# Two layers of attention and experts: products of the identity in front of instructions that TensorE waits for

## The chip, the cores and the metric

The kernel runs on one core of one Trainium2 chip. The metric is the device time of one execution in microseconds (us), as a median of several runs. A profile of one execution stands beside it. In the text, PE is TensorE, DVE is VectorE, ACT is ScalarE, POOL is GpSimd and SP is SyncE. "L1247" is line 1247 of the kernel before the change.

## What is computed

Two transformer layers follow each other on an input of 4 batches, 1024 rows and 256 columns, in float32. Each layer is an attention and a mixture of experts, both with a norm, a shift, a scale and a gate from a small modulation product. Cut to what matters:

```python
x = x + ga * attention0(norm(x) * (1 + ca) + sa)      # 16 heads, causal softmax, latent k and v
x = x + gb * experts0(norm(x) * (1 + cb) + sb)        # 16 experts, the best 2 of each row
x = x + ga1 * attention1(norm(x) * (1 + ca1) + sa1)   # linear attention with cubed q and k, a convolution of 3 rows
x = x + gb1 * experts1(norm(x) * (1 + cb1) + sb1)     # 8 experts, the best one of each row

def experts0(x):   # the reference computes all experts and picks two
    h = gelu(norm(x @ W1[e] + b1[e]) * g1[e] + be1[e])
    return sum(weight[e] * (h @ W2[e] + b2[e]) for e in best_two)
```

## The kernel before

The kernel does not compute all experts. It sorts the rows by expert: rows are written to DRAM, scattered by POOL's indirect DMAs into tiles of 128 rows that all belong to one expert, multiplied by that expert's weights, and gathered back. The tile's expert is a number in a register, so the weight is addressed at run time.

The stages follow each other as attention 0, experts 0, attention 1, experts 1. They overlap: what an object called `Around` holds (norms, routing, sorting, scattering, combining, each a Python generator cut into pieces) is traced in small pieces between the matmuls of the running stage. `k.around.step(pieces)` takes some pieces. A compiler then orders each engine's instructions by a schedule of its own, earlier code first among what is ready. `k.pin(ins)` fixes one order: the instruction stands behind the one that was traced last on the same engine. Each engine runs its instructions in that order.

Results of TensorE go to tiles in PSUM. A pool gives a tag a number of buffers; a new tile takes the buffer of an old one and waits until all readers of the old tile are done.

What the change touches:

- `Sorting.sort` ranks the rows of each expert (`ps_rank`, L895, read by DVE at L899 and L901). DVE then works out where each expert's tiles begin (L904 to L947). A product `ps_expert` (L949) counts the experts before each tile, and DVE turns that into an offset (L950). It serves both layers: in experts 0 for two halves of the batches (`hf`), in experts 1 for three parts (`p`: batches 0 and 1, batch 2, batch 3).
- `routed_rows` normalises a batch for the experts: ACT or DVE write `h` (L1030 to L1046), TensorE transposes it (`ps_lnT`, L1057), ACT copies it (L1063 or L1068), and `route_logits` multiplies by the router (L794) and turns the logits (L802, read at L803).
- `Experts0.run` walks through 22 groups of 4 tiles, 11 of each half. For a group, `arrive` transposes the sorted rows (`ps_xT`, L1224, copied by ACT at L1230). `hidden` multiplies by W1 (`ps_h`, L1247), and DVE adds the bias and takes the statistics (L1255 to L1263). `normalised` is on ACT (L1270). `turned` transposes (`ps_hT`, L1286) and applies the gelu on ACT (L1295). `output` multiplies by W2 (`ps_y`, L1312), and DVE adds the bias (L1321). Each tag has 2 buffers, and a group takes two of them. In a round, `turned` of group n-2, `hidden` of group n, `arrive` of group n+1 and `output` of group n-2 are traced in this order. At the switch to the second half (`second_half`), `arrive` comes after `output`, since the rows must have been scattered. The pools for `ps_xT` also serve `k.misc` (`ps_lnT`, `ps_route`, `ps_logits`, `ps_rank`, `ps_expert`).
- `attention1` runs `front(b)` and `back(b-1)` side by side. `front` transposes the norm (`ps_lnT`, L153), multiplies by the weights of k and v (`ps_k`, L1511) and of q (`ps_q`, L1537). `back` has `ps_o` (L1574), its transposes `ps_oT` (L1589), the convolution (L1597 on ACT, L1601 on DVE) and the projection `ps_pr` (L1609). The norms and sorts of experts 1 are traced in pieces between them.

Of the kernel before, what the change touches and what calls it, by code (L numbers as in the profile page):

```python
# [8 lines left out]
F32 = mybir.dt.float32  # L9
# [6 lines left out]
P = 128  # L16
# [49 lines left out]
def bcast(ap, axis, n):  # L66

    shape = list(ap.shape)
    shape.insert(axis, n)
    return ap.unsqueeze(axis).to_broadcast(shape)  # L70

# [771 lines left out]
class Sorting:  # L843
# [38 lines left out]
    def sort(self, sel, pool, index, offset):  # L882
# [65 lines left out]
        pe = k.misc.tile([1, self.tiles], F32, tag="m", name="ps_expert")  # L948
        nc.tensor.matmul(pe, lhsT=self.all[:ne, 0:1], rhs=past[:, 1], start=True, stop=True)  # L949
# [67 lines left out]
def routed_rows(k, work, b, statistics, scale, shift, wr, br, ne, logits, scalar):  # L1017


    nc = k.nc  # L1020
# [31 lines left out]
    for q in range(2):  # L1052
        hT = work.tile([P, CC, 512], F32, tag="hT", name="hT", bufs=1)
        for cc in range(CC):
            ps = k.misc.tile([P, 512], F32, tag="m", name="ps_lnT")
            for i in range(4):
                tr = nc.tensor.transpose(  # L1057
                    ps[:, i * P : (i + 1) * P], h[:, i, cc * P : (cc + 1) * P], k.ident
                )
                if i == 0:  # L1060
                    k.pin(tr)
            if scale is None:
                nc.scalar.activation(  # L1063
                    hT[:, cc], ps, AF.Identity,
                    bias=k.modF[:, cc, b : b + 1], scale=k.modF[:, 2 + cc, b : b + 1],
                )
            else:
                nc.scalar.copy(hT[:, cc], ps)  # L1068
            if q == 0 and cc == CC - 1:
                h = yield from normalised(1)  # L1070
            else:
                yield 1
        yield from route_logits(k, hT, wr, br, ne, work, logits[:, 4 * q : 4 * q + 4])


class Experts0:
# [40 lines left out]
    def sort(self, hf):  # L1117

        k, rt, keep, sorting, logits = self.k, self.rt, self.keep, self.sorting, self.logits
        nc = k.nc  # L1120
# [57 lines left out]
    def run(self, early):  # L1178
# [37 lines left out]
        def arrive(tiles, xss):  # L1216

            xTs = []
            for i, xs in zip(range(0, len(tiles), 2), xss):
                m = min(2, len(tiles) - i)  # L1220
                ps = ps_x.tile([P, 2, CC, P], F32, tag="m", name="ps_xT")
                for j in range(m):
                    for cc in range(CC):
                        tr = nc.tensor.transpose(  # L1224
                            ps[:, j, cc], xs[:, j, cc * P : (cc + 1) * P], k.ident
                        )
                        if j == cc == 0:
                            k.pin(tr)
# [5 lines left out]
        def hidden(hf, tiles, xTs):  # L1234
# [7 lines left out]
            for i in range(0, n, 2):  # L1242
                m = min(2, n - i)
                ph = ps_h.tile([P, 2, C], F32, tag="h", name="ps_h")
                for j in range(m):
# [58 lines left out]
        def output(hf, tiles, at, acts):  # L1304

            n = len(tiles)
            for i in range(0, n, 2):
                m = min(2, n - i)
                po = ps_o.tile([P, 2, C], F32, tag="o", name="ps_y")
                for j in range(m):  # L1310
# [43 lines left out]
        for n, (hf, tiles) in enumerate(groups):  # L1354
            last = waiting.pop(0) if len(waiting) > 1 else None

            if last and n > 2:
                acts = turned(*last)
            now = hidden(hf, tiles, xTs)
# [6 lines left out]
            switch = n + 1 == most  # L1366
            if n + 1 < len(groups) and not switch:
                xTs = arrive(groups[n + 1][1], coming.pop(0))
# [10 lines left out]
            if switch:  # L1379
                xTs = arrive(groups[n + 1][1], coming.pop(0))  # L1380
# [8 lines left out]
        normalised(*final)  # L1389
        output(*last[:3], acts)  # L1390
# [54 lines left out]
def attention1(ctx, k, a, after_batch=lambda b: None):  # L1445
# [48 lines left out]
    def front(b):  # L1494
# [13 lines left out]
        for t in range(NT):  # L1508
            ps = ps_p.tile([P, 512], F32, tag="p", name="ps_k")
            for cc in range(CC):  # L1510
                k.anchor = nc.tensor.matmul(  # L1511
                    ps, lhsT=hT[:, cc, t * P : (t + 1) * P], rhs=wqkv[:, cc, C:],
                    start=cc == 0, stop=cc == CC - 1,
                ).ins
# [269 lines left out]
class Experts1:  # L1784
# [42 lines left out]
    def rows(self, b):  # L1827

        k, rt = self.k, self.rt
        part = next(p for p in PARTS if b in p)  # L1830
# [15 lines left out]
    def sort(self, p):  # L1846

        k, rt, keep, sorting, logits = self.k, self.rt, self.keep, self.sortings[p], self.logits
# [169 lines left out]
def two_layers(ctx: ExitStack, tc: tile.TileContext, a: dict, out: bass.AP):  # L2018
# [56 lines left out]
    def stages(first, second, early):  # L2075
        for buffer in k.sorted0 + k.sorted1:
            buffer.writers.clear()
        k.around, k.statistics, k.xn, k.anchor = Around(), {}, None, None
# [108 lines left out]
```

## Time and profile before

| | us |
|---|---|
| median of 3 runs | 1098.98 |
| lowest and highest run | 1098.36, 1101.94 |
| the profiled execution | 1087.63 |
| its span, from the first to the last instruction | 1085.8 |

| engine | busy us | share of the span |
|---|---|---|
| PE | 945.7 | 87% |
| DVE | 620.4 | 57% |
| ACT | 602.5 | 55% |
| POOL | 336.0 | 31% |

The mean granted clock of TensorE is 0.955 of full speed. Attention 0 takes the span up to some 515 us, experts 0 goes to 749, attention 1 to 970, experts 1 to the end.

In lines of the timeline, the first two numbers are start and length in us, then come engine, line, operation, output and inputs, shapes and the number of records. In brackets stand the idle time of the engine before it and what ended that. In lines of stretches, the first numbers are the stretch and its length, then the busy time of PE, PE's weight loads, DVE, ACT and POOL with their records, then the granted clock, the share of the DMA engines and GB/s.

### The profile page before, as it was taken

How to read it: one execution, taken by the hardware profiler on the slowest of the kernel's cores; microseconds unless marked ns; L12 is line 12 of the kernel's file. 1: busy time of each engine (PE TensorE's matmuls, PEld its weight loads, DVE VectorE, ACT ScalarE, POOL GpSimd, SP SyncE). 2: the span in 40 equal slices, each digit the busy share in tenths (PEclk: the TensorE clock that was granted, in tenths of full speed). 3: DMA queues.
4: the chain of work that ended last, by engine and by line, in shares of the span. 5: the costliest groups of instructions: out<-in, count | busy, mean ns of one | idle time of the engine just before them, and what ended most of it. 6: DMA issues, size and time to landing. Idle time of an engine off the chain costs nothing.

```text
span 1085.8 us, 18090 instructions
## 1 busy us (share of the span) xinstructions
PE 945.7 (87%) x6072; PEld 559.8 (52%) x6072; DVE 620.4 (57%) x1987; ACT 602.5 (55%) x959; POOL 336.0 (31%) x528
## 2 busy tenths in 40 slices
PE   4899999999999999889679989986997989858760
PEld 2434434443443434335568878874464656547550
DVE  5822235422465155413676767993899968564572
ACT  0368655765477555775555657766654745523430
POOL 2013211311232234663004615612550100553632
PEclk9999999999999999999899999998999899989875
DMA  6995000100010001552825556624223201458764
GB/s 206 358 346 179 1 1 6 40 1 1 1 64 1 1 30 54 201 215 78 317 88 170 197 177 189 196 75 144 67 65 148 88 2 39 141 170 264 240 205 130
DMA packets 97142, 132.89 MB, mean 122 GB/s; under 512 B 8536, under 2 KB 84216, under 8 KB 96528
## 3 DMA queue, kind: packets, MB, share of 16 engines
q1 hardware_dynamic: 84656, 97.27, 26.9%
q0 software_dynamic: 11776, 33.57, 9.9%
q8 instruction: 52, 0.85, 0.3%
q10 hardware_dynamic: 608, 0.79, 0.3%
q14 instruction: 50, 0.41, 0.1%
HBM read 67.85 MB, written 63.75 MB: 121 GB/s over the span
## 4 chain that ended last, share of the span: by engine, by line
PE 63%; DVE 19%; issue 5%; DMA 5%; ACT 4%; POOL 1%; SPq 1%; DVEq 0%; ACTq 0%; POOLq 0%
PE ps_s L388 13%; PE ps_av L453 12%; PE ps_qk L364 6%; PE ps_y L1312 5%; PE ps_h L1247 4%; PE ps_v L349 3%; PE ps_out L427 3%; PE ps_pr L1609 3%; PE ps_y L1938 3%; PE ps_q L1537 2%; PE ps_k L1511 2%; DVE y L1601 2%; DMA ys<-results,index 2%; PE ps_lnT L1057 1%; DVE st L1258 1%
## 5 line engine op out<-in xcount | busy, mean ns | idle before, releaser
L396 ACT ACTIVATE pT<-ps_s 128x1024 f32<-128x1024 f32 x288 | 279.3, 1022 | 169.7 <-PE ps_s L388 167.2
L399 POOL TENSOR_SCALAR_AFFINE_SELECT pT<-pT 128x256 f32<-128x256 f32 x256 | 104.2, 431 | 328.4 <-ACT pT L396 323.7
L388 PE MATMUL ps_s<-qT,kT 32*128 32x512 f32 (+3 forms) x1536 | 178.8, 523 | 0.1
L453 PE MATMUL ps_av<-pT,v 128*32 128x512 f32 (+3 forms) x1536 | 165.2, 497 | 9.4 <-DVE turned L411 5.6
L964 POOL DMA_INDIRECT sorted<-hs,index x96 | 96.2, 1002 | 144.9 <-PE ps_y L1312 73.0
L974 POOL DMA_INDIRECT ys<-results,index x96 | 102.7, 1070 | 119.0 <-DMA results<-y 43.6
L388 PEld LDWEIGHTS ps_s<-qT,kT 32*128 32x128 f32 x1536 | 74.5, 185 | 95.5 <-issue 72.8
L453 PEld LDWEIGHTS ps_av<-pT,v 128*32 128x32 f32 x1536 | 40.6, 108 | 104.0 <-issue 58.7
L1247 PE MATMUL ps_h<-w,xT 128*128 x352 | 82.1, 386 | 6.5 <-DVE mv L1259 3.8
L1312 PE MATMUL ps_y<-w,act 128*128 x352 | 83.7, 392 | 4.2 <-DVE rs_seed L84 2.8
L411 DVE STREAM_TRANSPOSE turned<-ps_av 128x512 f32<-128x512 f32 x32 | 22.8, 712 | 98.9 <-PE ps_av L453 98.6
L1312 PEld LDWEIGHTS ps_y<-w,act 128*128 128x128 f32 x352 | 67.7, 197 | 14.0 <-ACT act L1295 4.8
L1247 PEld LDWEIGHTS ps_h<-w,xT 128*128 128x128 f32 x352 | 66.2, 193 | 15.9 <-issue 4.2
L1295 ACT ACTIVATE act<-ps_hT,gain 128x128 f32<-128x128 f32 x176 | 63.6, 463 | 16.9 <-PE ps_hT L1286 16.8
L1270 ACT ACTIVATE hid<-hid,nmr,rstd 128x256 f32<-128x256 f32 x88 | 47.5, 603 | 39.4 <-DVE nmr L1263 39.2
L1511 PE MATMUL ps_k<-wqkv,hT 128*128 128x512 f32 x128 | 61.9, 603 | 3.6 <-DMA wqkv<-in_wqkv_dram 2.8
L1938 PE MATMUL ps_y<-we,xT 128*128 x200 | 53.0, 412 | 10.6 <-ACT xT L1930 8.4
L371 DVE COPY qT<-ps_qk 128x512 f32<-128x512 f32 x16 | 11.0, 688 | 81.8 <-PE ps_qk L364 81.8
L103 DVE BATCH_NORM_STATS2 ln_st<-x 128x6 f32<-128x256 f32 x128 | 49.2, 407 | 0.5
L1255 DVE TENSOR_TENSOR hid<-ps_h,b 128x256 f32<-128x256 f32 x88 | 33.9, 415 | 26.6 <-PE ps_h L1247 21.5
L1938 PEld LDWEIGHTS ps_y<-we,xT 128*128 128x128 f32 x200 | 38.2, 204 | 20.1 <-ACT xT L1930 11.6
L374 DVE TENSOR_SCALAR kT<-ps_qk,par 128x512 f32<-128x512 f32 x32 | 22.5, 745 | 37.0 <-PE ps_qk L364 37.0
(223 smaller groups left out, 1499.4 us busy)
## 6 DMA issues: line engine op xcount, KB each, us to landing
xs<-sorted SPq DMA_DIRECT2D x69, 256.0 KB, 3.8
results<-y SPq DMA_DIRECT2D x69, 256.0 KB, 3.0
sorted<-zero SPq DMA_DIRECT2D x2, 6016.0 KB, 20.1
rows_in<-h SPq DMA_DIRECT2D x16, 512.0 KB, 2.9
hs<-rows_in POOLq DMA_DIRECT2D x32, 256.0 KB, 3.5
w<-in_w_dram SPq DMA_DIRECT2D x8, 1024.0 KB, 11.3
x<-in_x_dram SPq DMA_DIRECT2D x4, 1024.0 KB, 6.5
b<-in_b_dram SPq DMA_DIRECT2D x2, 2048.0 KB
```

The costliest lines, as they stand in the source:

```text
L364: nc.tensor.matmul(ps, lhsT=w[:, cc, g * P : (g + 1) * P], rhs=hT[:, cc, hf * 512 : (hf + 1) * 512], start=cc == 0, stop=cc == CC - 1,)
L388: k.anchor = nc.tensor.matmul(pair[hh // 2][:, hh % 2, c0 : c0 + w], lhsT=kTs[o][rows, kb * P : (kb + 1) * P], rhs=qT[rows, q1 - w : q1], ...
L396: nc.scalar.activation(pT, ps, AF.Exp, scale=1.0 / L**0.5)
L399: nc.gpsimd.affine_select(out=pT[:, :, c0 : c0 + P], in_=pT[:, :, c0 : c0 + P], compare_op=ALU.is_ge, fill=0.0, base=0, pattern=[[0, 2], [ ...
L453: nc.tensor.matmul(po[32 * hh : 32 * hh + 32, 512 - w :], lhsT=vs[b % 2][:, kb, 8 * g + 2 * hh + o, :], rhs=exps[b, g, o, u][hh // 2][:, h ...
L964: i = self.k.nc.gpsimd.indirect_dma_start(out=buffer.ap, out_offset=bass.IndirectOffsetOnAxis(ap=index, axis=0), in_=rows, in_offset=None, ...
L974: self.paced(self.k.nc.gpsimd.indirect_dma_start(out=rows, out_offset=None, in_=buffer.ap, in_offset=bass.IndirectOffsetOnAxis(ap=index, a ...
L1247: mm = nc.tensor.matmul(ph[:, j], lhsT=xTs[i // 2][:, j, cc], rhs=w1[:, cc, bass.ds(at[i + j], C)], start=cc == 0, stop=cc == CC - 1,)
L1295: o = nc.scalar.activation(act[:, j, cc], pt[:, j, cc], AF.Gelu, bias=gain[:, 1, cc, t : t + 1], scale=gain[:, 0, cc, t : t + 1],)
L1312: mm = nc.tensor.matmul(po[:, j], lhsT=acts[i // 2][:, j, cc], rhs=w2[:, cc, bass.ds(at[i + j], C)], start=cc == 0, stop=cc == CC - 1,)
L1511: k.anchor = nc.tensor.matmul(ps, lhsT=hT[:, cc, t * P : (t + 1) * P], rhs=wqkv[:, cc, C:], start=cc == 0, stop=cc == CC - 1,).ins
L1938: k.anchor = nc.tensor.matmul(po[:, j], lhsT=xT[:, j, cc], rhs=self.we[:, cc, bass.ds(at[j], C)], start=cc == 0, stop=cc == CC - 1,).ins
```

## The change

A function `keep_warm` issues n products of the identity with itself into a PSUM tile that a following instruction then overwrites, so nobody reads them. The first is pinned. A dictionary `k.fill` holds how many are wanted under a name; the place that takes the number removes it. The code sets 16 and 20 in front of `ps_expert` of the second sort of each layer, 18, 12, 5 and 5 in front of the first `ps_lnT` of each batch for experts 1, 13 in front of `ps_h` of group 1, 12 and 9 in front of `ps_xT` of group 4 and of the first group of the second half, 9 in front of `ps_y` of the last group but one, and 10 in front of the first `ps_k`. The tile of `ps_expert` becomes 128 by 128, of which the first row is used as before. `ps_expert` in all sorts and the first `ps_k` are pinned.

```diff
--- before.py
+++ after.py
@@ -68,6 +68,15 @@
     shape = list(ap.shape)
     shape.insert(axis, n)
     return ap.unsqueeze(axis).to_broadcast(shape)
+
+
+def keep_warm(k, ps, n):
+
+
+    for i in range(n):
+        mm = k.nc.tensor.matmul(ps, lhsT=k.ident, rhs=k.ident, start=True, stop=True)
+        if i == 0:
+            k.pin(mm)
 
 
 def rsqrt(nc, pool, out, var, n, eps):
@@ -945,8 +954,10 @@
             nc.vector.tensor_scalar(past[:, i], self.numbers, edge[:, i : i + 1], None, ALU.is_ge)
         mine = pool.tile([ne, self.tiles], F32, tag="mine", name="mine")
         nc.vector.tensor_tensor(mine, past[:, 0], past[:, 1], ALU.subtract)
-        pe = k.misc.tile([1, self.tiles], F32, tag="m", name="ps_expert")
-        nc.tensor.matmul(pe, lhsT=self.all[:ne, 0:1], rhs=past[:, 1], start=True, stop=True)
+        pe = k.misc.tile([P, P], F32, tag="m", name="ps_expert")
+        keep_warm(k, pe, k.fill.pop("expert", 0))
+        pe = pe[0:1, : self.tiles]
+        k.pin(nc.tensor.matmul(pe, lhsT=self.all[:ne, 0:1], rhs=past[:, 1], start=True, stop=True))
         nc.vector.tensor_scalar(offset, pe, float(ne - 1), float(C), ALU.min, ALU.mult)
         yield 1
         return mine
@@ -1053,6 +1064,8 @@
         hT = work.tile([P, CC, 512], F32, tag="hT", name="hT", bufs=1)
         for cc in range(CC):
             ps = k.misc.tile([P, 512], F32, tag="m", name="ps_lnT")
+            if q == cc == 0:
+                keep_warm(k, ps[:, :P], k.fill.pop("rows", 0))
             for i in range(4):
                 tr = nc.tensor.transpose(
                     ps[:, i * P : (i + 1) * P], h[:, i, cc * P : (cc + 1) * P], k.ident
@@ -1116,6 +1129,8 @@
 
     def sort(self, hf):
 
+        if hf == 1:
+            self.k.fill["expert"] = 16
         k, rt, keep, sorting, logits = self.k, self.rt, self.keep, self.sorting, self.logits
         nc = k.nc
         sel = rt.tile([P, 2, HT, E0], F32, tag="sel", name="sel")
@@ -1219,6 +1234,7 @@
             for i, xs in zip(range(0, len(tiles), 2), xss):
                 m = min(2, len(tiles) - i)
                 ps = ps_x.tile([P, 2, CC, P], F32, tag="m", name="ps_xT")
+                keep_warm(k, ps[:, 0, 0], k.fill.pop("rows of tiles", 0))
                 for j in range(m):
                     for cc in range(CC):
                         tr = nc.tensor.transpose(
@@ -1242,6 +1258,7 @@
             for i in range(0, n, 2):
                 m = min(2, n - i)
                 ph = ps_h.tile([P, 2, C], F32, tag="h", name="ps_h")
+                keep_warm(k, ph[:, 0, :P], k.fill.pop("hidden", 0))
                 for j in range(m):
                     for cc in range(CC):
                         mm = nc.tensor.matmul(
@@ -1307,6 +1324,7 @@
             for i in range(0, n, 2):
                 m = min(2, n - i)
                 po = ps_o.tile([P, 2, C], F32, tag="o", name="ps_y")
+                keep_warm(k, po[:, 0, :P], k.fill.pop("output", 0))
                 for j in range(m):
                     for cc in range(CC):
                         mm = nc.tensor.matmul(
@@ -1356,6 +1374,8 @@
 
             if last and n > 2:
                 acts = turned(*last)
+            if n == 1:
+                k.fill["hidden"] = 13
             now = hidden(hf, tiles, xTs)
             if last and n == 2:
                 acts = turned(*last)
@@ -1364,6 +1384,8 @@
             if n:
                 k.around.step()
             switch = n + 1 == most
+            if n == 3:
+                k.fill["rows of tiles"] = 12
             if n + 1 < len(groups) and not switch:
                 xTs = arrive(groups[n + 1][1], coming.pop(0))
             if switch:
@@ -1377,6 +1399,7 @@
             if last:
                 output(*last[:3], acts)
             if switch:
+                k.fill["rows of tiles"] = 9
                 xTs = arrive(groups[n + 1][1], coming.pop(0))
             if n == most + 1:
                 k.around.tasks.append(self.combine(0))
@@ -1387,6 +1410,7 @@
         last, final = waiting
         acts = turned(*last)
         normalised(*final)
+        k.fill["output"] = 9
         output(*last[:3], acts)
         output(*final[:3], turned(*final))
         k.around.finish_tasks()
@@ -1507,11 +1531,16 @@
         waiting = []
         for t in range(NT):
             ps = ps_p.tile([P, 512], F32, tag="p", name="ps_k")
+            if b == t == 0:
+                keep_warm(k, ps[:, :P], 10)
             for cc in range(CC):
-                k.anchor = nc.tensor.matmul(
+                mm = nc.tensor.matmul(
                     ps, lhsT=hT[:, cc, t * P : (t + 1) * P], rhs=wqkv[:, cc, C:],
                     start=cc == 0, stop=cc == CC - 1,
-                ).ins
+                )
+                if b == t == cc == 0:
+                    k.pin(mm)
+                k.anchor = mm.ins
             r = work.tile([P, C], F32, tag="r", name="r", bufs=3)
             k3 = work.tile([P, C], F32, tag="k3", name="k3", bufs=3)
             cube(k3, ps[:, :C], r)
@@ -1827,6 +1856,7 @@
     def rows(self, b):
 
         k, rt = self.k, self.rt
+        k.fill["rows"] = (18, 12, 5, 5)[b]
         part = next(p for p in PARTS if b in p)
         i = b - part[0]
         if i == 0:
@@ -1845,6 +1875,8 @@
 
     def sort(self, p):
 
+        if p == 1:
+            self.k.fill["expert"] = 20
         k, rt, keep, sorting, logits = self.k, self.rt, self.keep, self.sortings[p], self.logits
         nc = k.nc
         nt = sorting.nt
@@ -2075,7 +2107,7 @@
     def stages(first, second, early):
         for buffer in k.sorted0 + k.sorted1:
             buffer.writers.clear()
-        k.around, k.statistics, k.xn, k.anchor = Around(), {}, None, None
+        k.around, k.statistics, k.xn, k.anchor, k.fill = Around(), {}, None, None, {}
         k.fits = [k.good[:, 3 + i : 4 + i] for i in range(SORTS)] if early else None
         experts0 = Experts0(k, a)
 
```

## The prediction, made before the change was run

> **What bounds the kernel.** First the page: engine shares, granted clock, shares of the chain that ended last.
>
> ```profile
> PE 945.7 (87%) x6072; PEld 559.8 (52%) x6072; DVE 620.4 (57%) x1987; ACT 602.5 (55%) x959; POOL 336.0 (31%) x528
> PEclk9999999999999999999899999998999899989875
> PE 63%; DVE 19%; issue 5%; DMA 5%; ACT 4%; POOL 1%; SPq 1%; DVEq 0%; ACTq 0%; POOLq 0%
> ```
>
> TensorE carries 63% of the chain, at full clock nearly everywhere. The clock falls only in single slices. Next, TensorE's waits (total, times, longest); the change aims at these:
>
> ```profile
> PE ps_expert L949 <- DVE index L933: 7.7, 1, 7.7
> PE ps_expert L949 <- DVE past L945: 6.6, 4, 4.8
> PE ps_lnT L1057 <- DVE ln_nmr L126: 5.7, 1, 5.7
> PE ps_h L1247 <- DVE mv L1259: 3.8, 1, 3.8
> PE ps_y L1312 <- DVE rs_seed L84: 2.8, 1, 2.8
> ```
>
> Third, busy time by stretches around some gaps; the clock is the number after POOL's:
>
> ```profile
> 519.70:523.50 3.80, 0.03 (x1) 0.00 (x0) 3.46 (x7) 1.26 (x3) 0.00 (x0) 1.00 1.05 414
> 523.90:527.10 3.20, 3.20 (x9) 2.57 (x8) 1.40 (x6) 0.00 (x0) 0.00 (x0) 0.50 1.03 410
> 480.60:484.00 3.40, 3.40 (x32) 1.19 (x32) 0.00 (x0) 0.92 (x1) 3.05 (x7) 1.00 0.21 76
> 633.10:636.40 3.30, 3.14 (x15) 3.17 (x16) 0.00 (x0) 1.42 (x3) 0.00 (x0) 0.50 0.92 263
> ```
>
> An idle TensorE is followed by half clock: after the 3.82 us before 523.54, and after the 2.86 us before 633.26. It is not after the 2.24 us that ended at 480.51. One such stretch costs little: 16 records of ps_h take 5.38 us at 523.54 and 3.72 at 515.14, so 1.66 us. Fourth, the timeline where two of the fills go, and where the fill for batch 2 goes:
>
> ```profile
> 522.99 0.41 DVE L1255 TENSOR_TENSOR hid<-ps_h,b 128x256 f32<-128x256 f32 x1
> 523.54 5.38 PE L1247 MATMUL ps_h<-w,xT 128*128 x16 [3.82 <-DVE mv L1259]
> ...
> 737.94 0.42 DVE L1321 TENSOR_TENSOR y<-ps_y,b 128x256 f32<-128x256 f32 x1
> 738.51 5.38 PE L1312 MATMUL ps_y<-w,act 128*128 x16 [2.83 <-DVE rs_seed L84]
> ...
> 936.79 1.63 PE L1574 MATMUL ps_o<-kv,qT 128*128 128x136 f32 x12
> 940.37 0.60 PE L1057 MATMUL ps_lnT<-ident,h 128*128 128x128 f32 x4
> ```
>
> At 523.54 TensorE starts just after VectorE's second read of an old ps_h (ends 523.40), though both input copies (ACT, L1230) ended by 520.96. With two ps_h buffers this is a wait for the **buffer**, not for the input. The same at 738.51: the second L1321 ends at 738.36, while the first activations were there by 736.6. So the wait covers both reads of the tile.
>
> **The price of a product.** No identity product is in the trace. The nearest row is ps_o (L1574): 12 records of 136 columns in 1.63 us, the last taking 0.28, so (1.63 - 0.28) / 11 = 0.12, in its even runs 0.116; for 128 columns 0.109. The code's two products per ps_o leave four records, so a product is two records: 0.22 us, 0.43 at half clock. Lower end 0.11, if it went like a transpose (L1224: 8 in 1.04). I take 0.22. The 129 products are 28 us of TensorE time, against gaps of about 40 us.
>
> **The change, place by place.** A fill writes the tile of the instruction behind it, so it needs the same buffer and starts no earlier than the buffer is free. Plus is slower.
>
> - *hidden, 13* (523.54). Buffer wait: fills start at 523.5, not in the gap. Half clock comes at 523.8 anyway. 1 product at 0.22, 8 at 0.43 until 527.2, 4 at 0.22: end 528.0. Then 16 records at 0.216 instead of the half-clock ones: end 531.5, against 528.76. **+2.8**. VectorE then idles for ps_h already (1.83 us before 527.14) and everything to 535 hangs on it, so nothing absorbs it.
> - *output, 9* (738.51): likewise. Fills to 742.0, ps_y to 745.6 against 743.72: **+1.9**, on the path into layer 1, as SyncE's loads there are queued behind the last results.
> - *rows of tiles, 12*, at group 4 (554.27). The 3.55 us wait of this line (541.28) belongs to group 3, so no gap is met. 2.6 us of fills replace a 1.15 us wait; the 1.57 us wait at 565.15 hides the rest, unless the fills also go ahead of ps_logits (554.16), which the sort on VectorE waits for (then +1.4). Between 0 and 1.4; **+0.5**.
> - *expert, 16*, first half's end (571.98, gap 4.85). The fills are pinned behind hidden's matmuls (end 563.59), not behind ps_rank (565.15) or ps_hT. In the gap as meant they end at 570.6 and ps_xT and ps_y run at full clock (1.97 to 1.04, and 2.42 to 1.92), 0.2 of it lost to a buffer: -1.2. All ahead of ps_rank they take 3.5 us where 1.57 is free: +1.9. Near the middle: **+0.3**.
> - *rows of tiles, 9*, at the switch (633.26, waits for a DMA, buffer long free): ends 632.3. Saves 0.9 + 0.7 on the two rows of 8 transposes (1.94 and 1.76, against 1.04). The start of half-clock stretches is not tied to the program; gaps this near the limit will drop in some runs only: **-0.9**, between -1.6 and 0.
> - *ps_k, 10* (756.18, waits for wqkv). Pinned behind all 16 ps_lnT, of which 6 now run after ps_k. They move into the gap, fills follow from 755.3: end 757.5 at full, 759.6 at half clock. First ps_k 1.3 to 3.4 us later, but those 6 (1.45) are done and ACT had not read it before 760.40: between -0.4 and +1.1; **+0.2**.
> - *rows 18 and 12* (842.13, 894.89): they end at 840.4 and 894.0, in the gaps, and keep the clock. But ACT is busy without a gap from 842.10 to 850 and from 895.56 to 902; it paces these stretches: **0**, between -1 and +0.5.
> - *rows 5, 5*. Batch 2 (940.37): TensorE has come straight from ps_o, no gap, and ACT L1063 sat idle 0.71 us for this tile: 5 x 0.22 = **+1.1**. Batch 3 (974.30, gap 1.72): **0**.
> - *expert, 20* (960.40, gap 7.67): 4.4 us leave 3.3 idle, enough to drop the clock again. Keeping it would save half of 3.7 us of ps_pr: 1.8. **-0.5**.
>
> Pins of ps_expert and ps_k remove freedom of order elsewhere; bounds +1 and -1, taken 0. Sum: 2.8 + 1.9 + 0.5 + 0.3 - 0.9 + 0.2 + 0 + 1.1 - 0.5 = +5.4 us. The profiled execution took 1087.63 us for a span of 1085.8, so the sum makes it 1093.0. The median of the runs, 1098.98, is 11.35 higher; I carry the difference over: 1104.4.
>
> **A rule against the trace.** After gaps of 2.83 and 2.86 us the trace has clock 0.50; after 2.24 it has 1.00. The Trainium skill ("TensorE: Matmul & The Clock Gate", "Why this matters for your kernels") tells to avoid idle over about 3 us; by that the gap at the switch would never drop the clock, its gain would be nothing and the sum +6.3. The measured rows decide. The same page's Part 4 says that transposes don't count as busy for the clock. Here the stretch from 633.10 has 15 records, all transposes, at 0.50, and the next 16 matmuls took 3.62 us, full speed. By the page the two rows at the switch would hold the clock low one stretch longer and the gain there would be 3 us; the trace decides.
>
> **Rivals.** *As meant (faster).* Every fill runs while TensorE waits, and the half-clock costs go: 1.7 + 1.2 + 1.6 + 1.7 + 1.7 + 1.8 = 9.7 us, less 1.1 for batch 2: 1090. It decides if fills at hidden and output start at 519.7 and 735.7. For it: the gaps are there and the clock does fall. Against: the buffer reads at 523.40 and 738.36. *Nothing net.* VectorE and ACT pace the stretches behind the fills, and half of the buffer delays vanishes there: 1099.5. *Order (much slower).* Products with no operand to wait for are put ahead of unready instructions: ps_rank, ps_logits, ps_lnT; +1.9, +1.4, +1.1 at their upper ends and the gains gone: 2.8 + 1.9 + 1.4 + 1.9 + 1.1 + 1.1 + 1 = 11.2: 1110. *It does not do what it says*: the clock still drops behind filled gaps, because these products count too little; 1107, part of the slower side.
>
> **Numbers.** Forecast 0.48 (its own range 1100 to 1109), as meant 0.22, nothing net 0.15, order and no effect 0.15. 0.3% is 3.3 us, about what a measurement of this kernel can tell from no change. Above 1102.3: 0.38 of the first and the last group, 0.53; below 1095.7: 0.23; between: 0.24. Range 1091 to 1111.
>
> **What would show it.** In the changed profile, fills on ps_h and ps_y that start after VectorE's second read, followed by ps_h at full clock that ends near 531.5 after a 515 start; the switch's transposes at about 1.04 us; ps_lnT of batch 2 a microsecond after ps_o. Wrong, if those fills start with the gap, or if ps_y behind them is early; the order rival shows in where ps_rank and ps_logits stand.

## The result, and the profile of the changed kernel

Changed 1099.62 us, before 1098.66 us (medians of 20 runs each), ratio 1.0012, 95% interval 0.9995 to 1.003: +1.0 us, between -0.5 and +3.3. No change that this measurement can tell; the forecast was 5.4 us slower. In two later comparisons the changed kernel was 5.3 and 5.4 us slower by the medians (e9, e13 below). In some comparisons all kernels, before included, run about 10 us shorter (before 1087 instead of 1098; one and the same chip gave 1086.69 and 1096.55). So only kernels of one comparison are set against each other. The profile of before that the prediction read (1087.63) was of the short sort, and the 11.35 us that the prediction carried over are this difference. Why the first comparison gave +1.0 and the two later ones +5.3 and +5.4 stays open.

The profiled execution of the changed kernel took 1100.96 us, its span 1099.1. Its page: engine shares, clock, shares of the chain.

```profile
PE 978.9 (89%) x6330; PEld 590.8 (54%) x6330; DVE 621.2 (57%) x1987; ACT 603.0 (55%) x959; POOL 336.0 (31%) x528
PEclk9999999999999999999999999998999899989885
PE 69%; DVE 15%; issue 5%; ACT 4%; DMA 4%; POOL 1%; another core or an unknown queue 1%; SPq 0%; DVEq 0%; POOLq 0%; ACTq 0%
```

258 matmul records more, all of them fills (129 products of two records), and 33 us of TensorE time. TensorE's waits, in the order of those shown of before (total, times, longest):

```profile
PE ps_expert L960 <- DVE past L954: 2.6, 4, 1.2
PE ps_lnT L1070 <- ACT h L1041: 4.0, 1, 4.0
PE ps_h L77 <- DVE hid L1272: 3.7, 1, 3.7
PE ps_y L77 <- DVE y L1339: 2.7, 1, 2.7
PE ps_kv L1526 <- DVE v L1551: 2.4, 1, 2.4
```

The long waits in front of ps_expert are gone: 7.7 and 4.8 us became at most 1.2. The waits in front of ps_h and ps_y are as long as before (3.8 and 2.8), but now it is the fill (L77) that waits in them. A wait of 2.4 us in front of ps_kv is longer than it was. The timeline at these places:

```profile
567.37 1.04 PE L1303 MATMUL ps_hT<-ident,hid 128*128 128x128 f32 x8
568.25 3.74 PE L77 MATMUL ps_expert<-ident 128*128 128x128 f32 x32
573.14 0.23 PE L960 MATMUL ps_expert<-past,all 16*1 16x44 f32 x2 [1.16 <-DVE past L954]
...
524.67 3.17 PE L77 MATMUL ps_h<-ident 128*128 128x128 f32 x26 [3.72 <-DVE hid L1272]
527.68 3.62 PE L1264 MATMUL ps_h<-w,xT 128*128 x16
...
745.10 3.67 PE L77 MATMUL ps_y<-ident 128*128 128x128 f32 x18 [2.74 <-DVE y L1339]
748.61 3.62 PE L1330 MATMUL ps_y<-w,act 128*128 x16
```

Ahead of ps_expert the fill stands in the gap, behind ps_hT. At hidden and output it starts only when the buffer is free, as the prediction said. Busy time and clock (the number after POOL's) in three stretches:

```profile
524.70:527.80 3.10, 3.10 (x27) 3.10 (x28) 2.84 (x14) 0.00 (x0) 0.00 (x0) 1.00 1.02 408
640.10:642.10 2.00, 1.86 (x16) 1.65 (x17) 0.00 (x0) 2.00 (x6) 0.00 (x0) 1.00 1.08 350
745.10:748.60 3.50, 3.50 (x18) 3.50 (x19) 1.95 (x12) 1.27 (x3) 0.00 (x0) 0.58 0.45 150
```

At hidden no half clock followed here, although TensorE had been idle for 3.72 us; at the switch (second row) the clock was kept; at output it was not.

Because executions differ by several us, the text goes by stretches, each between the starts of two matmul records (ps_y[16] is the 17th record that writes ps_y; records of fills are not counted). Us, in brackets us of half clock inside, all read from the traces:

| stretch | before | e1: before again | changed | e9: changed | e13: changed | e15 (the best version below) |
|---|---|---|---|---|---|---|
| ps_h[0] to ps_hT[0] (hidden 13) | 19.54 (3) | 19.10 (3) | 21.07 (0) | 22.74 (7) | 22.73 (7) | 19.46 (3) |
| ps_hT[0] to ps_y[16] (group 4) | 21.84 (3) | 21.83 (3) | 21.99 (3) | 23.02 (7) | 23.01 (7) | 21.81 (3) |
| ps_y[16] to ps_gain[8] (expert 16) | 19.80 (3) | 20.03 (3) | 17.07 (0) | 17.07 (0) | 17.09 (0) | 18.75 (0) |
| ps_gain[8] to ps_y[112] (untouched) | 42.68 (0) | 45.58 (0) | 46.17 (0) | 46.19 (0) | 45.78 (0) | 45.78 (0) |
| ps_y[304] to ps_y[336] (output 9) | 14.79 (3) | 16.15 (7) | 16.44 (3) | 16.38 (3) | 16.69 (3) | 13.10 (0) |
| ps_y[336] to ps_k[36] (ps_k 10, pin) | 45.86 (7) | 46.40 (7) | 47.86 (7) | 47.84 (7) | 49.44 (6) | 46.86 (10) |
| ps_kv[63] to ps_kv[90] (batch 0) | 52.91 (10) | 52.93 (10) | 53.98 (10) | 54.06 (10) | 53.36 (7) | 53.40 (14) |
| ps_kv[90] to ps_k[99] (batch 1) | 25.02 (3) | 25.03 (3) | 24.01 (0) | 24.02 (0) | 24.01 (0) | 24.01 (0) |
| ps_kv[126] to ps_rank[12] (batch 2) | 18.13 (0) | 18.30 (0) | 18.35 (0) | 18.34 (0) | 18.34 (0) | 18.23 (0) |
| ps_rank[12] to ps_y[416] (expert 20, batch 3) | 47.35 (10) | 47.25 (10) | 47.57 (7) | 46.60 (7) | 46.67 (4) | 43.94 (0) |

The fourth row, a stretch without fills, shows the two sorts of comparison: 42.7 us in every trace of the short one, 44.3 to 47.2 in those of the other.

### The profile page after: what moved, and what is told of

It is laid out like the page before. It is cut to its first block, busy times and chain, and to the rows that moved or that the text cites. A ratio compares the mean times of both kernels' runs of the same rounds, so it can differ in the third digit from the quotient of the medians.

```text
span 1099.1 us, 18603 instructions
## 1 busy us (share of the span) xinstructions
PE 978.9 (89%) x6330; PEld 590.8 (54%) x6330; DVE 621.2 (57%) x1987; ACT 603.0 (55%) x959; POOL 336.0 (31%) x528
## 4 chain that ended last, share of the span: by engine, by line
PE 69%; DVE 15%; issue 5%; ACT 4%; DMA 4%; POOL 1%; another core or an unknown queue 1%; SPq 0%; DVEq 0%; POOLq 0%; ACTq 0%
PE ps_s L397 14%; PE ps_av L462 13%; PE ps_y L1330 6%; PE ps_h L1264 5%; PE ps_qk L373 5%; PE ps_k L1537 4%; PE ps_out L436 3%; PE ps_pr L1638 3%; PE ps_v L358 2%; PE ps_q L1566 2%; PE ps_y L1970 2%; PE ps_lnT L1070 1%; PE ps_hT L1303 1%; PE ps_xT L1240 1%; DVE ln_st L112 1%
## 5 line engine op out<-in xcount | busy, mean ns | idle before, releaser
L1287 ACT ACTIVATE hid<-hid,nmr,rstd 128x256 f32<-128x256 f32 x88 | 47.6, 602 | 55.0 <-DVE nmr L1280 43.5
L1970 PE MATMUL ps_y<-we,xT 128*128 x200 | 55.2, 422 | 13.2 <-issue 6.5
L1339 DVE TENSOR_TENSOR y<-ps_y,b 128x256 f32<-128x256 f32 x88 | 35.2, 418 | 20.8 <-PE ps_y L1330 14.2
```

The lines of the kernel that those rows point to most:

```text
L1970: k.anchor = nc.tensor.matmul(po[:, j], lhsT=xT[:, j, cc], rhs=self.we[:, cc, bass.ds(at[j], C)], start=cc == 0, stop=cc == CC - 1,).ins
```

## The experiments

Every variant is cut from the changed kernel; "off" means a count of 0. Gains and losses are against before in the same comparison: difference of the medians, then the ratio with its interval. In the recorded expectations "forecast" is the prediction, and "working theory" what seemed likely by then.

**First set: the noise, the pins, and hidden alone.**

e1 is the kernel before, unchanged. 

> The kernel before, unchanged. Theory (the profiled execution of before, 1087.63 us, was an unusually short one): this profile comes out near the median, 1095 to 1102 us, with half-clock stretches of TensorE at other times than in the first profile and with some waits of ScalarE or TensorE that the program does not explain; landmarks of the two executions of one program differ by several us. Rival (executions of one program agree, and the 13 us between the two profiles belong to the change): 1087 to 1089 us with the same waits at the same places.

Measured 1097.69 against 1097.98 (ratio 0.9995, 0.9975 to 1.0016), its profiled execution 1099.21. The first expectation held. In the untouched stretch its timeline on VectorE shows a stop that the same program does not have in the first profile (1.17 us of idle time in front of the same instruction there):

```profile
592.04 0.42 DVE L1255 TENSOR_TENSOR hid<-ps_h,b 128x256 f32<-128x256 f32 x1 [5.25 <-PE ps_y L1312]
```

This instruction reads a ps_h whose last matmul had ended by 589.4; in the short sort VectorE stands idle for 1.4 us in front of the same one (e6). So two single profiles cannot be set against each other in sum.

e2 sets all counts to 0 and leaves the pins:

```diff
-            k.fill["hidden"] = 13        (and all other counts)
+            k.fill["hidden"] = 0
```

> All fills set to 0; what stays of the change are the two pins, on ps_expert and on the first ps_k. Working theory: the pins cost nothing, the median is 1098.7 within 1.5 us. Rival (pins take freedom from the order of work): 1 us or more slower, with ps_q or ps_k of layer 1 later against the landmarks before them than in the kernel before.

1099.82, +1.8 us (1.0018, 1.0001 to 1.0035): by the median the rival held, by the interval the loss lies between 0.1 and 3.8 us. In its trace the order of instructions differs from that of before only around the first ps_k (756 to 773 us), on TensorE, VectorE and ScalarE; the pin on ps_expert changes no order. VectorE and then TensorE:

```profile
768.85 1.22 DVE L1623 TENSOR_TENSOR x<-x,bg 128x1024 f32<-128x1024 f32 x1
...
770.32 1.22 DVE L1623 TENSOR_TENSOR x<-x,bg 128x1024 f32<-128x1024 f32 x1
771.45 0.41 DVE L1548 TENSOR_REDUCE recs<-k 128x16 f32<-128x256 f32 x1
```

```profile
773.04 0.73 PE L1526 MATMUL ps_kv<-v,k 128*128 128x136 f32 x4 [2.21 <-DVE v L1551]
```

Two x<-x,bg of 1.22 us stand ahead of the first sum that ps_kv needs; in e1 it is one, and ps_kv waits 1.03 us:

```profile
769.24 1.22 DVE L1594 TENSOR_TENSOR x<-x,bg 128x1024 f32<-128x1024 f32 x1
770.37 0.41 DVE L1519 TENSOR_REDUCE recs<-k 128x16 f32<-128x256 f32 x1
```

```profile
771.96 0.73 PE L1502 MATMUL ps_kv<-v,k 128*128 128x136 f32 x4 [1.03 <-DVE v L1522]
```

The stretch ps_y[336] to ps_k[36] took 47.67 us in e2, 10 of them at half clock. Traces without this pin took 46.86 to 47.31 where they also had 10 us of half clock, and 45.86 to 46.67 where they had 7. So 0.4 to 0.8 us are order; the rest of the 1.3 us to e1 (46.40, 7 at half clock) goes with the clock.

e3 and e4 keep hidden's fill alone, 13 products in e3 and 52 in e4; all other counts are 0, and both pins are off:

```diff
-        k.pin(nc.tensor.matmul(pe, lhsT=self.all[:ne, 0:1], rhs=past[:, 1], start=True, stop=True))
+        nc.tensor.matmul(pe, lhsT=self.all[:ne, 0:1], rhs=past[:, 1], start=True, stop=True)
-                if b == t == cc == 0:
-                    k.pin(mm)
```

> Only the 13 products in front of ps_h of the second tile group's hidden layer, without the two pins. Forecast's step: ps_h behind the fill ends 2.8 us later and everything after it too, median 1101.5. Working theory (the delay is taken up by the 3.6 us wait in front of the next ps_xT, which another engine ends): the 16th ps_h 2.9 us later, the first ps_y behind it at most 0.5 us later, median 1098.7 within 1.5 us. As meant: the fill runs in the gap and both are earlier by 1.7 us.

> The same fill four times as long, 52 products, alone. Price of 0.22 us each and nothing taken up: 11.3 us later at ps_h, at the first ps_y and at the end, median 1110. Working theory (about 3 us are taken up behind it): 11.3 us later at ps_h, about 8 us at the first ps_y and at the end, median 1106.5 to 1107.5. If each product cost one record only (0.11 us): ps_h 5.5 us later, the end 2.5 us.

e3: +0.1 us by the medians (1.001, 0.9987 to 1.0032); ps_h[0] to ps_hT[0] took 21.87, 2.8 longer than in e1, and to ps_gain[8] 64.00 against 60.96. So it was not taken up in front of ps_xT, as the working theory said; the sum of the run doesn't tell 0 from 2.8. e4: +11.1 us (1.0112, 1.0086 to 1.0138), what the forecast's price gives if nothing is taken up (11.3). TensorE's wait in front of ps_rank is the one that could have taken the delay up. It is as long in e3 as in before (1.57), and 1.58 in e4:

```profile
566.60 0.67 PE L904 MATMUL ps_rank<-some,before 128*128 128x256 f32 x2 [1.57 <-DVE mv L1276]
```

The price itself, in the timeline of e4:

```profile
521.87 14.34 PE L77 MATMUL ps_h<-ident 128*128 128x128 f32 x104 [3.72 <-DVE hid L1272]
536.05 3.62 PE L1264 MATMUL ps_h<-w,xT 128*128 x16
```

104 records for 52 products; at 0.109 us each 11.4 us, and 2.6 more for the 5.2 us of half clock inside: 14.0.

**Second set: parts of the change** (the short sort, before 1086.69).

```diff
e5:  hidden 13, rows of tiles 12, expert 16; all others off, no pin on ps_k
e6:  expert 16; all others off, no pin on ps_k
e7:  the changed kernel with
-    keep_warm(k, ps[:, :P], 10)
-                if b == t == cc == 0:
-                    k.pin(mm)
e8:  hidden, output, rows of tiles at group 4, batch 2 and ps_k off, no pin on ps_k
```

> Only the three fills of the first half's end: hidden 13, rows of tiles 12 at group 4, expert 16. From the first ps_h to ps_gain[8] the kernel before takes 61.2 us (60.96 and 60.81 in the two executions after it), the changed kernel 60.1. Working theory (the forecast's +3.6 for these three did not arrive: the delay at hidden is taken up by the waits in front of ps_rank, and the fill ahead of ps_expert keeps the clock): 60.1 here, median 1097 within 1.5. Forecast: 64.8 here, median 1102. If the fill at hidden passes on as it does alone (64.0): 62 to 64 here and a median of 1099 to 1101.

> Only the 16 products in front of the first half's ps_expert. Working theory: from ps_y[16] to ps_gain[8] 17.1 us as in the changed kernel, where the kernel before takes 19.8 to 20.0; 2.8 us earlier, median 1095.5 to 1097. As meant in the prediction: 1.2 us earlier. Forecast: 0.3 later, 20.2 us. Fills put ahead of ps_rank: 1.9 later. If the switch behind it, which waits for GpSimd's scatters, starts from ps_expert too, the gain lasts to the end; if it starts from something else, it is gone at the switch and the median is 1098.5.

> The changed kernel without the ten products on ps_k and without the pin on it. Working theory (the pin, not the products, puts VectorE's two x<-x,bg in front of the sums that ps_kv waits for, about 2 us, and the products cost 1.4 us more): 2 to 3.4 us faster than the changed kernel, median 1096 to 1098; from ps_y[336] to ps_k[36] 45.8 us, as in the kernel before, where the changed one takes 47.9. Forecast (ps_k costs 0.2, pins nothing): 1099.4 and no difference.

> Only the fills in gaps that no buffer closes: expert 16 and 20, rows of tiles 9 at the switch, rows 18, 12 and 5 for batches 0, 1 and 3; without hidden, output, rows of tiles at group 4, batch 2 and ps_k with its pin. Working theory, from the stretches of the changed kernel: expert 16 -2.8, switch -0.9, batch 1 -1.0, the rest 0: 1094 within 1.5. Forecast's own terms: +0.3 -0.9 +0 -0.5 = -1.1: 1097.6. Rival (whatever is gained here is lost again in front of the next transfer or at the switch): 1098.7, no difference from before.

e5: -0.2 us (0.9997, 0.9983 to 1.0012); from ps_h[0] to ps_gain[8] 61.8 us against 61.2: neither the forecast's 64.8 nor 60.1. e6: -1.4 us (0.997, 0.9955 to 0.9986); ps_y[16] to ps_gain[8] 18.75, 1.05 shorter: near the as-meant 1.2, not the working theory's 2.8. The 17.07 of the changed kernel are 1.7 us less, as much as TensorE's wait in front of ps_rank (1.57). That wait is there in every trace without the fill at group 4, e3, e4 and e11 with hidden's fill among them, and gone in all six with it. So it is the fill at group 4 whose delay ends there, not that at hidden. (VectorE's order in front of ps_rank is another one in these six; which of the two ended the wait was not separated.) e7: -2.2 us (0.9972, 0.9954 to 0.9989), where the changed kernel was 1.0 and, later, 5 us slower than before, in other comparisons. The stretch ps_y[336] to ps_k[36] took 46.7 (45.8 expected), 1.2 us less than in the changed kernel. The stretch ps_rank[12] to ps_y[416], which e7 does not touch, took 43.34 without any half clock, 3.3 to 4.2 us less than in the changed kernel's three traces. So e7's sum is not the price of the place ps_k. e8: -4.4 us (0.994, 0.9919 to 0.9961): the working theory's 4.7, not the forecast's 1.1.

**Third set: the buffer.** e9 is the changed kernel; e10 moves two fills to other tiles:

```diff
-                keep_warm(k, ph[:, 0, :P], k.fill.pop("hidden", 0))
+                spare = ps_o.tile([P, 2, C], F32, tag="o", name="ps_spare")
+                (13 times) nc.tensor.matmul(spare[:, 0, :P], lhsT=xTs[0][:, 0, 0], rhs=k.ident, ...)
-                keep_warm(k, po[:, 0, :P], k.fill.pop("output", 0))
+                spare = ps_h.tile([P, 2, C], F32, tag="h", name="ps_spare")
+                keep_warm(k, spare[:, 0, :P], k.fill.pop("output"))
e11: these two, with expert 16 and 20, the switch's 9, rows 12 and 5 for batches 1 and 3
e12: expert 20; all others off, no pin on ps_k
```

> The changed kernel once more, beside its variants on one chip. Working theory: 1 us slower than before, within 2; stretches: first ps_h to ps_hT[0] 2 us longer, ps_y[16] to ps_gain[8] 2.7 shorter, ps_y[304] to ps_y[336] 1.8 longer, ps_y[336] to ps_k[36] 1.5 to 2 longer, ps_kv[63] to ps_k[72] 1 longer, ps_kv[90] to ps_k[99] 1.0 shorter, ps_rank[12] to ps_y[416] 3 to 4 shorter unless half clock falls into it. Forecast: 5.4 slower.

> The changed kernel with the two buffer-bound fills written to a tile that nobody holds: hidden's 13 products (of xT with the identity, so that they come after the transposes) into a ps_y buffer, output's 9 into a ps_h buffer; everything else, the order on TensorE too, as in the changed kernel. Theory (the buffer, not the products, kept them out of the gap): hidden's products start 2 to 3 us earlier, near 520.5, ps_h starts when its buffer is free at full clock, first ps_h to ps_hT[0] about 17.9 us against 21 to 22.8, and ps_y[304] to ps_y[336] about 13.2 us against 16.4 to 16.7; the kernel 5 to 8 us faster than the changed one. Rival (products cost TensorE's time wherever they stand, or the clock drops all the same): no faster than the changed kernel by more than 1 us.

> Candidate for the best version: the gap fills of e8 without batch 0's 18, plus hidden 13 and output 9 in free tiles as in e10; no rows of tiles at group 4, no batch 2, no ps_k and no pin on it. Working theory: e8's gain (4.4 to 6.5 us) plus 1.7 at each of the two gaps plus 0.5 for batch 0: 8 to 10 us faster than before. Rival (the stretches behind are paced by VectorE and by transfers, so that the gaps' gain ends there): as e8, 4 to 6.

> Only the 20 products ahead of layer 1's last ps_expert. Working theory (with the fill in the order, four ps_pr are put into the gap too, ahead of ps_expert, so that work and not only the clock is gained): ps_rank[12] to ps_pr[99] 2.6 to 3.8 us shorter than the 9.9 of before, ps_rank[12] to ps_y[416] 2.5 to 4 shorter than 47.3, median 2 to 4 us faster than before. Forecast: 0.5 faster. Rival (ps_lnT of batch 3 behind it waits for ScalarE and gives it back): shorter at ps_pr[99], 47.3 to ps_y[416], no difference in the median.

e9: +5.3 us (1.0063, 1.004 to 1.0085). e10: -1.5 us against before (0.999, 0.9967 to 1.0013), 6.8 faster than e9. Its timeline at output, to be set beside 745.10 above:

```profile
741.35 2.17 PE L77 MATMUL ps_spare<-ident 128*128 128x128 f32 x18
744.35 3.69 PE L1339 MATMUL ps_y<-w,act 128*128 x16 [0.82 <-DVE rs_seed L93]
```

The products run in the gap at 0.12 us a record, ps_y starts when its buffer is free, at full clock: the stretch takes 13.10 (13.2 expected), 3.3 us less than in e9. At hidden the same was done and nothing came of it (TensorE, then ScalarE):

```profile
519.82 3.17 PE L1264 MATMUL ps_spare<-ident,xT 128*128 128x128 f32 x26 [0.81 <-ACT xT L1246]
522.82 3.63 PE L1271 MATMUL ps_h<-w,xT 128*128 x16
...
529.88 0.66 PE L1240 MATMUL ps_xT<-ident,xs 128*128 128x128 f32 x4 [2.55 <-ACT hT L1081]
```

```profile
527.28 2.08 ACT L1294 ACTIVATE hid<-hid,nmr,rstd 128x256 f32<-128x256 f32 x4 [7.04 <-DVE nmr L1287]
```

ps_h ran in the gap's end at full clock, and then TensorE waited 2.55 us for ScalarE's copy hT, which stands behind four instructions that wait for VectorE's small steps up to nmr (ends 527.25). ps_h[0] to ps_hT[0] took 22.02, where 17.9 were expected. In before, without a fill, ScalarE has the other order:

```profile
529.40 0.59 ACT L1068 COPY hT<-ps_lnT 128x512 f32<-128x512 f32 x1 [8.43 <-PE ps_lnT L1057]
...
531.42 2.07 ACT L1270 ACTIVATE hid<-hid,nmr,rstd 128x256 f32<-128x256 f32 x4
```

In e3, e10, e11 and the changed kernel, all with a fill at hidden, those four stand ahead of the copy. So the fill changed the order on ScalarE, and the wait of 2.55 us comes with it. What the fill would gain in the old order was not tried. e11: -0.8 us (0.9993, 0.9965 to 1.002): neither expectation. e12: +1.3 us (1.001, 0.9984 to 1.0037); its stretch to ps_pr[99] took 6.58 as expected, against 9.9, and to ps_y[416] 46.47, 0.8 of the 3.3 left: the rival.

**Fourth set: the best version.**

```diff
e13: the changed kernel          e14: the kernel of e8
e15: expert 16 and 20, the switch's 9, rows 12 for batch 1, output's 9 in a ps_h buffer; all others off, no pin on ps_k
e16: e15 with
-            self.k.fill["expert"] = 20
+            self.k.fill["expert"] = 0
```

> The changed kernel for the third time, beside e14 to e16. Working theory: 1 to 6 us slower than before, most likely 3; stretches as in e9.

> The kernel of e8 in the same call as the changed kernel. Working theory (the fills in open gaps gain, the other four places lose): 2 to 6 us faster than before and 6 to 9 us faster than the changed kernel. Rival (e8's gain belonged to its call): no faster than before, and within 3 us of the changed kernel.

> Candidate: expert 16 and 20, rows of tiles 9 at the switch, rows 12 for batch 1, and output's 9 in a free ps_h buffer; nothing else. Working theory, stretch by stretch: -1.1 (ps_y[16] to ps_gain[8]), -0.9 (switch), -1.7 (ps_y[304] to ps_y[336], 13.1 us), -1.0 (ps_kv[90] to ps_k[99]), -1 (ps_rank[12] to ps_y[416]): 4 to 6 us faster than before, 1 to 2 faster than e14. Rival (stalls and transfers behind them take it back): as e14 or before.

> e15 without the 20 products ahead of layer 1's last ps_expert. Working theory (that fill gains 2.6 us up to ps_pr[99] and gives back 1.5 to 2 of it in ps_y[368] to ps_y[416]): 0.5 to 1.5 us slower than e15. Rival (it gains nothing in all, or costs, since transfers start later): as fast as e15 or faster. By the 2.6 us of its stretch: 2.6 slower.

e13: +5.4 us (1.0044, 1.0017 to 1.0072). e14: +0.1 us (0.9986, 0.9953 to 1.0019), not e8's gain. **e15: 1090.90 against 1097.99, -7.1 us (0.9932, 0.9903 to 0.9962), faster than before and 12.5 us faster than the changed kernel.** e16: -4.7 us (0.9954, 0.9924 to 0.9983), 2.4 slower than e15 where 0.5 to 1.5 were expected. In e14 a stop like that of e1 stands on ScalarE, in front of a copy whose ps_xT had ended by 978.24 (VectorE's ln_mv, which the second row's instruction needs, ended at 979.88). In e15 ScalarE starts h at 973.69, as soon as ln_mv is there; a stop of VectorE of 2.83 us comes behind it (at 976.49). e14:

```profile
982.51 0.59 ACT L1957 COPY xT<-ps_xT 128x512 f32<-128x512 f32 x1 [7.38 <-remote]
982.99 2.08 ACT L1041 ACTIVATE h<-x,ln_mv,ln_rstd 128x256 f32<-128x256 f32 x4
```

In e8, the same program in the short sort:

```profile
970.73 0.59 ACT L1957 COPY xT<-ps_xT 128x512 f32<-128x512 f32 x1 [3.15 <-PE ps_xT L1953]
```

**Last set** (the short sort, before 1087.79): two fills put back into e15.

```diff
e17: self.k.fill["rows"] of batch 3 = 5        e18: of batch 0 = 18
```

> e15 with the five products in front of batch 3's rows put back. Working theory (the fill moves batch 3's ps_lnT and ps_xT on TensorE, and ScalarE's copy behind it): ps_rank[12] to ps_y[416] 46 to 47.5 us against 43.9 in e15, 2 to 4 us slower than e15. Forecast (0 for batch 3): as e15, 6 to 8 us faster than before.

> e15 with the 18 products in front of batch 0's rows put back. Working theory (the products take the gap, but with them ps_oT and ps_lnT stand in another order): ps_kv[63] to ps_k[72] 29.3 to 30.4 us against 28.5 to 29.0, then 0.45 less to ps_kv[90]: 0.4 to 1 us slower than e15. Forecast: 0, as e15.

e17: -8.1 us (0.9923, 0.9896 to 0.9951), e18: -7.5 us (0.9928, 0.9899 to 0.9956). Neither costs what can be told by the sum, though e15 itself did not run beside them; e17's stretch took 44.7 us, not the 46 to 47.5 expected, e18's came as expected (30.19, then 23.96 against 24.41). So in the short sort these two fills are no visible part of the 7.2 us between e14 and e15; 1.7 are output's, some 2.7 lie at the stop of ScalarE above (ps_lnT behind it waits 4.11 us in e14, 1.41 in e15), the rest is open.

## Why the prediction was wrong, step by step

The forecast was 5.4 us slower and said "clearly slower" with 0.53; the measurement says +1.0. "Nothing net" at 1099.5 came out by its number only: the delays at the two buffers did not halve behind them, as it had assumed. The steps that failed are terms of the sum: expert 16 (+0.3 said, a gain of 1.1 to 1.3 measured), group 4 (+0.5 said, -0.4 where it can be isolated), batch 2 (+1.1 said, +0.1), and three places at which the fill or the pin changed the order of instructions, which the sum put at nothing or weighed by the clock alone: ps_k with its pin (+0.2 said, +1.7 to +3.3), batch 1 (0 said, -1.0) and expert 20 (-0.5 said, up to -3.4). Against before and e1, by the stretches (changed, e9, e13):

- **Hidden 13, group 4 and expert 16 together: forecast +3.6, measured -0.9, +1.8, +1.8.** This is where the first measurement parted from the forecast. Hidden's own delay was right, and in the main "nothing absorbs it" too: against e1 it is 2.8 us at ps_hT[0] and 3.0 at ps_gain[8] in e3, 12.3 and 11.4 in e4, and the wait in front of ps_rank stays. Group 4 was too dear: the prediction named the wait of 1.57 us that "hides the rest" and charged +0.5 all the same. With its fill the wait is gone. e10 against e11, which have the same half clock up to ps_gain[8] and differ there in this fill alone: 38.15 against 38.55 us from ps_hT[0], so -0.4. What is left of the difference is the clock: "half clock comes at 523.8 anyway" holds in e9 and e13, not in the changed kernel's first profile: 13.6 us of half clock in these three stretches against 3.4, and 2.7 us between them in time.
- **Expert 16: forecast +0.3, measured -1.05 alone** (-1.3 against e1). The prediction weighed whether the fill is put ahead of ps_rank or into the gap, and took the middle. It stands in the gap, as meant. The middle of two cases was a value that neither could give.
- **The pins: forecast 0, measured +1.8 by the sum of e2** (0.1 to 3.8), 0.4 to 0.8 by its stretch at equal half clock. The prediction gave bounds of 1 us either way and looked only at what ps_k itself waits for. The pin moved VectorE's order. With ps_k's products (+0.2 forecast) the place costs 1.7 to 3.3 us in the changed kernel.
- **Batch 2: forecast +1.1, measured 0 to +0.2:** the delay is gone by ps_rank[12]. **Batch 0: forecast 0**, measured +0.4 to +1.1 in the stretch, nothing that e18's sum shows. **Batch 1: forecast 0, measured -1.0** in every kernel with that fill. It is not the clock: e2 had no half clock in this stretch and took 25.03 all the same. It is the order, as the timelines of before and of e15 show:

```profile
894.89 0.63 PE L1057 MATMUL ps_lnT<-ident,h 128*128 128x128 f32 x4 [3.60 <-DVE h L1046]
895.36 1.41 PE L1589 MATMUL ps_oT<-ident,on 128*128 128x128 f32 x8
```

```profile
894.01 2.92 PE L77 MATMUL ps_lnT<-ident 128*128 128x128 f32 x24 [0.26 <-DVE on L1609]
896.76 0.93 PE L1618 MATMUL ps_oT<-ident,on 128*128 128x128 f32 x7
897.52 0.60 PE L1070 MATMUL ps_lnT<-ident,h 128*128 128x128 f32 x4
```

Seven ps_oT run in the gap behind the fill; without the fill they come behind the first ps_lnT.
- **Output 9: forecast +1.9, measured +1.6 to +1.9** against the 14.79 of before. That is the middle one of the ten traces without this fill, which go from 14.48 to 16.15; e1 is the longest, with 7 us of half clock, and against it the cost is 0.2 to 0.5. Right in the main, with its cause: e10 and e15 take the buffer away and gain 1.7.
- **Expert 20 and batch 3: forecast -0.5, measured +0.3 to -0.7** in the changed kernel, but -3.4 in e15. The prediction looked for the clock alone. The order shows more, in before and in the changed kernel:

```profile
960.40 0.20 PE L949 MATMUL ps_expert<-past,all 8*1 8x14 f32 x2 [7.67 <-DVE index L933]
960.54 8.94 PE L1609 MATMUL ps_pr<-wg,y 128*128 128x256 f32 x32
...
963.33 6.20 PE L77 MATMUL ps_expert<-ident 128*128 128x128 f32 x40
969.37 2.32 PE L1638 MATMUL ps_pr<-wg,y 128*128 128x256 f32 x10
971.62 0.20 PE L960 MATMUL ps_expert<-past,all 8*1 8x14 f32 x2
```

With the fill in its list, the order written at build time puts five ps_pr (10 records) in front of ps_expert, into what was the gap; before, all 32 records came behind. As at batch 1, that is work moved forward; here the clock gains beside it (half clock up to ps_pr[99]: 8.1 us in before, 3.4 in the changed kernel). How much of it reaches ps_y[416] depends on the sort of comparison: in the short one the four traces with this fill took 43.3 to 44.9 us and the three without 47.3 to 47.6; in the long one seven of the eight with it took 46.3 to 47.7, and e15 43.9, against 47.2 to 48.4 without.
- **The switch: forecast -0.9.** The clock was kept in the changed kernel (window 640.10, 1.00). In the long sort its worth can't be read, as ps_y[112] to ps_y[144], the stretch around it, took 21.93 us in before and 25.40 in e1, the same program. In the short sort it took 21.56 to 22.03 us in the three traces without the fill, each with 3.4 us of half clock, and 20.70 to 22.27 in the four with it, which have none: in the mean 0.2 us less. So the clock came as forecast, and hardly any time with it.

The touched stretches without the switch add up to +2.9, +4.6 and +5.9 us in the three executions (each against the mean of before and e1, output against 14.79), beside medians of +1.0, +5.3 and +5.4. The three profiled executions themselves lay 2.3, 4.4 and 2.2 us above before's medians, so the third sum does not account for its own execution. The sum of the forecast was near two of the medians because its errors cancel, which is luck: too much for batch 2, group 4 and expert 16, nothing for the pins, no gain at batch 1. Executions of one program differ by as much as the whole effect; 0.53 for "slower" left out that both the clock's phase and the stops described at the end change what the same program loses.

The rule weighed in the prediction (the Trainium skill, "TensorE: Matmul & The Clock Gate", "Why this matters for your kernels": no idle over about 3 us) is no threshold here. In e1 TensorE waited 2.23 us before 725.41, in e3 2.22 us before 726.12; then:

```profile
726.00:729.40 3.40, 3.40 (x10) 2.69 (x9) 3.40 (x7) 3.40 (x10) 0.00 (x0) 0.51 0.23 77
```

in e1, and in e3

```profile
726.10:729.50 3.40, 3.38 (x16) 2.99 (x17) 3.40 (x8) 3.40 (x10) 0.00 (x0) 1.00 0.23 77
```

The half-clock stretches of e1 between 500 and 730 us begin at 521.2, 538.3, 569.0, 637.3 and 726.0: 5, 9, 20 and 26 times 3.41 us apart. The same page's Part 1 says that the clock is judged in free-running windows of 3413 ns; these rows agree. In e1 the idle time before 725.41 lies inside one stretch of this grid (722.6 to 726.0); in e3, whose grid has a line at 724.8, it is cut in two. So a gap of 2.2 to 3.7 us drops the clock in one execution and not in the next, and a fill there has an expected worth, not a fixed one.

## What to carry to other kernels

A fill that keeps a clock up must be able to start when the gap starts: write it to a tile that nobody holds (output: some +1.7 us in the buffer of the instruction behind it, -1.7 in another). That alone is not enough (hidden gained nothing even then). Count a pin, or a fill, as a change of order on every engine, and compare the built orders before costing it: here order moved 0.4 to 2.6 us at places where only the clock or the buffer had been weighed (hidden, the pin, batch 1). Where executions of one program differ by as much as the effect, compare stretches of several traces rather than two sums, and repeat the comparison: the first one here was 4 us from the next two.

## What was not expected of the hardware

In the long sort of comparison VectorE and ScalarE stood still for 2.6 to 4.3 us although the matmuls that they waited for had ended by the trace, at places that differ from program to program (e1 at 592, e14 at 982). The trace's records of semaphores, by which one engine tells another that it is done, show what they waited for. In e1 TensorE's semaphore has no record between 585.56 and 591.94, then eight within 0.4 us, and VectorE starts at 592.04; in e6 the records come one by one, the one that is needed at 589.03, and VectorE starts at 589.12. In e14 TensorE's next record behind 976.70 stands at 982.48, and ScalarE starts at 982.51. Such bursts, five or more records within 0.4 us after a silence of over 1 us, are there 3 to 7 times in each of the 13 traces of the long sort and in none of the 7 of the short one. The long sort also has fewer records of this semaphore, 999 to 1018 against 1059 to 1070. So the signals come late, or are recorded late, in one sort only; why, the traces do not say.

One such stop is as long as the whole effect looked for here. How much of the 10 us between the two sorts they are was not measured, but most of the difference lies where they are: e1, with the same order of instructions as before on TensorE, VectorE and ScalarE, falls back by 7.1 us between 595 and 732 us and by another 4 near 1015.

It was not expected either that 0.22 us for a product of the identity, taken from a different instruction's row, would hold so closely (104 records in 14.34 us).
